# Six vector-engine exponentials per group, squared on GpSimd, in a one-core graph-attention kernel

## The chip, the cores and the metric

The kernel runs on one core of a Trainium2 chip. The core has TensorE (matmuls; the profile calls it PE, and its weight loads PEld), VectorE (DVE), ScalarE (ACT), GpSimd (POOL) and SyncE (SP, which here only issues DMAs). Each engine works through its own instruction list in order; semaphores order the engines among themselves. The metric is the device time of one execution in microseconds, and the median of several runs is quoted.

## The reference

Four layers work on a graph of 3,327 nodes with 128 features and a dense 3,327 x 3,327 matrix `adj`. Nearly all the time goes to the first layer, an attention with 128 heads of 8 elements each:

```python
q = (x @ Wq.T).reshape(d, n, h)          # d = 128 heads, n = 3327 nodes, h = 8
k = (x @ Wk.T).reshape(d, n, h)
v = (x @ Wv.T).reshape(d, n, h)
a = jnp.einsum('dnh,dmh->dnm', q, k) * d ** (-0.5)
a = a + adj + adj
a = softmax(a, axis=2)
out = einsum('dnm,dmh->dnh', a, v).reshape(n, h * d) @ Wo.T
```

So for every head and every pair of nodes there is one exponential: 128 x 3,327 x 3,327, some 1.4 billion. The other three layers multiply with `adj` a few times and take the last 800 us of the span.

## The kernel before

**Work and order.** The attention stage handles the nodes n in 7 chunks of up to 476 columns (`CW`), the heads in 32 groups of four (`NG`), and the nodes m in 26 tiles of 128, taken two at a time as 13 *pairs* per group (`q` = 0..12; rows `r` = 0 and 1 of a pair). That makes 7 x 32 = 224 groups and 2,912 pairs. The order of the instructions on every engine is written out by hand (`manual_schedule`): the loop over `i` at the end of the stage runs through *slots*, four to a pair, one for each head j. The index u counts pairs.

**Scores in place.** A pair owns two of seven PSUM banks of `S`. VectorE *seeds* a bank with adj minus a shift (`seed`, L645). TensorE adds the scores of head 0 (`scores`, L654), ScalarE takes exp(2x) of both rows in one instruction 952 columns wide (`exps`, L666), and then TensorE turns the bank from head j-1 to head j by adding q_j k_j - q_(j-1) k_(j-1), so that one seed serves four heads. For this `QS` holds q of head j beside the negated q of the head before. Every seventh pair has its banks at the two ends of the ring, and there ScalarE needs two instructions of 476 columns (L669) for each head. `values` (L713) multiplies the four heads' exponentials by V into bank `po`, two slots of matmuls after the last head.

**By hand.** In the pairs with q in `BY_HAND` = (0, 2, 5, 7, 10), *hand pairs* below, VectorE computes the exponential of row 1, head 0, by a polynomial, and ScalarE only does row 0 (476 columns) in that slot. `hand_exp` reads the raw score out of PSUM (L691, tile `h`), seeds the bank for the later heads (`seed(u, 1)`), and then runs four more instructions (L695 three times, L697), the last of which multiplies by `EA`, the exponential of adj minus shift. The loop spreads these: one in slot 3 of the hand pair, two in slot 0 of the next pair and one in its slot 3. A generator in `by_vector` holds the state. `heads_of` lets `values` use a hand-made exponential one pair later than the others.

**Other VectorE work.** In slot 1 the loop seeds row 1 of the *next* pair (`seed(u+1, 1)`), unless that is a hand pair, and in slot 2 row 0 of the pair after that. Both seeds of one bank wait until ScalarE has read the bank's former content. In slot 2 of the pair q = 2 the sums of the group before are copied out of `po` (`store`, L721). While the chunks run, 22 of the 26 squares of `adj` are also transposed piece by piece for later use (`Square`, `plan_squares`: L288, L292), three or four per chunk.

**Loads for the next group** (`loads`, on SP's queue): at q = 1 all keys (`load_k`, 16 DMAs into `KT`), q of head 0 (`load_q`) and V (`load_v`). At q = 3, 5 and 7 GpSimd negates q of head 0, 1 and 2 (`negate_q`, L570), and the next head's q is loaded over part of it. At q = 8 GpSimd spreads V (`spread_v`, L580) and reads one column of `KT` (`all_here`, L584), which the first scores of the next group wait for. In the last group of a chunk the next chunk's 26 tiles of `adj` are loaded too. GpSimd also issues the stores of the sums (L725).

## Time and profile before

| what | value |
|---|---|
| median of 3 runs | 10,983.07 us (10,979.53 to 10,989.63) |
| the profiled execution | 10,981.96 us, of which its span is 10,980.2 us |
| attention loop, first to last exponential | 462.5 to 10,168.1 us of the span |
| busy in that stretch: ACT, PE, DVE, POOL | 9,667.7, 9,609.5, 7,786.3, 1,290.0 us |
| granted TensorE clock in that stretch | 1.00 |
| DMA share in that stretch | 0.58, 96 GB/s |

A line of the page's costliest groups reads: source line, engine, operation, output tile <- input tiles, shapes, count | busy us, mean ns of one | idle time of that engine just before these instructions, and who ended it. The mean of one instruction contains its start and end, which overlap with the neighbours on ScalarE; what counts for the loop is the distance from start to start. A line of the timeline reads: start, length, engine, source line, operation, tiles, count, and in square brackets the idle time before it with who ended it; neighbouring instructions of one group are merged.

### The profile page before, as it was taken

The page shows a single profiled execution, that of the slowest core. Times are in us where ns is not written, and L with a number is a line of the kernel's source. Part 1 is how long each engine was busy: PE and PEld are TensorE (multiplying, and loading weights), DVE is VectorE, ACT ScalarE, POOL GpSimd, SP SyncE. Part 2 cuts the span into 40 slices and gives each one's busy share as a digit, 9 for nine tenths or more (in the row PEclk, how much of TensorE's full clock was granted, in tenths as well). Part 3 has the DMA queues.
Part 4 walks back from the last instruction along what each step waited for, and adds up shares of the span by engine and source line. Part 5 has one row for each costly group of instructions (what it writes and reads, how often), then busy time and mean ns, then how long its engine had stood idle before and what let it go on. Part 6 is the DMA issues. An engine that isn't in the chain of part 4 may idle for free. (4 is left out here: it accounts for less than half of the span.)

```text
span 10980.2 us, 204474 instructions
## 1 busy us (share of the span) xinstructions
PE 10533.5 (96%) x72876; PEld 3435.7 (31%) x72876; DVE 8487.1 (77%) x13503; ACT 10033.1 (91%) x13789; POOL 1529.1 (14%) x2477
## 2 busy tenths in 40 slices
PE   4599999999999999999999999999999999999889
PEld 2133333333333333333333333333323333333544
DVE  5588887888878887788887888878877777777655
ACT  3599999999999999999999999999999999999330
POOL 5011111111111111111111111111111111111101
PEclk7799999999999999999999999999999999999999
DMA  8766566565566565565556565565556555554668
GB/s 250 250 99 97 94 96 113 93 98 96 89 118 97 93 97 88 106 98 97 90 95 119 94 96 93 95 119 95 87 93 98 96 95 86 82 88 71 206 233 281
DMA packets 695339, 1256.98 MB, mean 114 GB/s; under 512 B 195218, under 2 KB 555049, under 8 KB 691244
## 3 DMA queue, kind: packets, MB, share of 16 engines
q1 hardware_dynamic: 644044, 1114.42, 55.7%
q0 software_dynamic: 50272, 129.37, 4.3%
q8 instruction: 587, 9.62, 0.4%
q14 instruction: 436, 3.57, 0.2%
HBM read 1096.53 MB, written 146.60 MB: 113 GB/s over the span
## 5 line engine op out<-in xcount | busy, mean ns | idle before, releaser
L666 ACT ACTIVATE e<-S 128x952 f32<-128x952 f32 (+1 forms) x9024 | 8357.9, 1099 | 36.7 <-PE S L654 29.4
L713 PE MATMUL po<-e,VA 128*9 128x476 f32 (+1 forms) x46592 | 5737.5, 564 | 33.0 <-DVE OS L721 12.3
L645 DVE TENSOR_TENSOR S<-a,shb 128x476 f32<-128x476 f32 (+1 forms) x5824 | 3937.9, 676 | 1447.6 <-ACT e L666 1059.4
L654 PE MATMUL S<-QS,KT 64*128 64x476 f32 (+1 forms) x22176 | 4528.6, 445 | 79.7 <-DMA a<-adjT 28.4
L654 PEld LDWEIGHTS S<-QS,KT 64*128 64x128 f32 x22176 | 2073.7, 184 | 5100.5 <-issue 1301.3
L669 ACT ACTIVATE e<-S 128x476 f32<-128x476 f32 (+1 forms) x4128 | 2467.5, 711 | 1.1 <-PE S L654 0.6
L695 DVE SCALAR_TENSOR_TENSOR e<-e,h 128x476 f32<-128x476 f32 (+1 forms) x2240 | 1497.8, 669 | 77.0
L713 PEld LDWEIGHTS po<-e,VA 128*9 128x9 f32 x46592 | 691.0, 88 | 1606.6 <-issue 1488.1
L570 POOL TENSOR_SCALAR QS<-QS 128x476 fp32r<-128x476 f32 (+1 forms) x672 | 485.6, 723 | 4312.1 <-DMA QS<-qS_d 2612.2
L725 POOL DMA_DIRECT2D oT_d<-OS x896 | 470.5, 530 | 3668.8 <-DVE OS L721 3625.5
L691 DVE TENSOR_SCALAR h<-S 128x476 f32<-128x476 f32 (+1 forms) x1120 | 728.0, 650 | 300.9 <-PE S L654 296.5
L697 DVE SCALAR_TENSOR_TENSOR e<-e,EA 128x476 f32<-128x476 f32 (+1 forms) x1120 | 759.6, 678 | 0.0
L695 DVE SCALAR_TENSOR_TENSOR e<-h 128x476 f32<-128x476 f32 (+1 forms) x1120 | 743.1, 663 | 0.0
L1107 PE MATMUL pu<-strip,y 128*128 128x512 f32 (+2 forms) x1456 | 600.5, 566 | 31.7 <-DVE y L968 14.8
L654 PE MATMUL S<-QZ,KT 64*128 64x476 f32 (+1 forms) x1120 | 493.4, 441 | 11.9 <-DVE S L645 10.5
L1107 PEld LDWEIGHTS pu<-strip,y 128*128 128x128 f32 (+1 forms) x1456 | 271.9, 191 | 305.8 <-issue 272.1
L1111 DVE TENSOR_REDUCE deg<-strip 128x1 f32<-128x1536 f32 (+1 forms) x104 | 193.8, 1881 | 63.7 <-DMA strip<-adjT 44.1
L580 POOL COPY VA<-VR 128x832 f32<-128x832 f32 x224 | 242.3, 1082 | 0.0
L654 PEld LDWEIGHTS S<-QZ,KT 64*128 64x128 f32 x1120 | 205.1, 183 | 92.2 <-DVE S L645 52.4
L288 DVE STREAM_TRANSPOSE cols<-rows 128x416 f32<-128x416 f32 x208 | 204.5, 988 | 30.3 <-DMA rows<-in_adj_dram 22.6
L1060 ACT COPY uT<-pu 128x512 f32<-128x512 f32 (+1 forms) x21 | 11.1, 555 | 222.6 <-PE pu L1107 222.6
L721 DVE COPY OS<-po 128x476 f32<-128x476 f32 (+1 forms) x224 | 146.3, 653 | 87.3 <-PE po L713 87.3
(255 smaller groups left out, 1958.6 us busy)
## 6 DMA issues: line engine op xcount, KB each, us to landing
KT<-kS_d SPq DMA_DIRECT2D x1792, 208.0 KB
KT<-kS_d SPq DMA_DIRECT2D x1792, 104.0 KB
VR<-v_d SPq DMA_DIRECT2D x224, 416.0 KB
QS<-qS_d SPq DMA_DIRECT2D x3072, 14.9 KB
QS<-qS_d SPq DMA_DIRECT2D x1536, 29.8 KB
adjT<-cols SPq DMA_DIRECT2D x26, 1664.0 KB
a<-adjT SPq DMA_DIRECT2D x156, 238.0 KB
strip<-adjT POOLq DMA_DIRECT2D x39, 895.5 KB, 5.1
```

The lines of the kernel that those rows point to most:

```text
L570: nc.gpsimd.tensor_scalar(QS[b][:, j + 1, :w], QS[b][:, j, :w].bitcast(F32), -1.0, 0.0, op0=ALU.mult, op1=ALU.add)
L580: nc.gpsimd.tensor_copy(VA[(c * NG + g) % 2][:, :, :, 0:H], v.rearrange("p j (t e) -> p t j e", e=H))
L645: touch(u, [r], nc.vector.tensor_tensor(bank(u, r), adj_of[c][2 * q + r][:, :w], shift_of[c][:, :w], op=ALU.subtract))
L654: x = nc.tensor.matmul(bank(u, r), KT[b][64 * r:64 * r + 64, max(0, j - 1), q * P:(q + 1) * P], q_s[64 * r:64 * r + 64, :w], start=hand an ...
L666: touch(u, (0, 1), nc.scalar.activation(e[:, :, :w], S[:, odd:even + 1, :w], AF.Exp, scale=2.0))
L669: touch(u, [r], nc.scalar.activation(e[:, 1 - r, :w], bank(u, r), AF.Exp, scale=2.0))
L691: touch(u, [1], nc.vector.tensor_scalar(s, bank(u, 1), EXP_ARG, None, op0=ALU.mult))
L695: nc.vector.scalar_tensor_tensor(e, s if k == 3 else e, EXP_C[k], s, op0=ALU.add, op1=ALU.mult)
L697: nc.vector.scalar_tensor_tensor(e, e, EXP_C[0], EA[pairs[u][2]][:, :w], op0=ALU.add, op1=ALU.mult)
L713: nc.tensor.matmul(po[32 * j:32 * j + H + 1, :w], VA[k % 2][:, 2 * pairs[v][2] + of, j, :], e_of[v, j][:, 1 - of, :w], start=(q == 0 and r ...
L725: nc.gpsimd.dma_start(oT_d[:, d * N + c * CW:d * N + c * CW + w], o[32 * j:32 * j + H + 1, :w])
L1107: nc.tensor.matmul(ps[:, :k], y[:m, t, :], s[:m, c * 4 * P - c0:c * 4 * P - c0 + k], start=(t == 0), stop=(t == NT - 1))
```

## The change

The hand pairs become q = 0, 2, 4, 6, 8 and 10, every second one. The polynomial has one VectorE instruction less: VectorE adds a constant while it reads the score (L691), GpSimd squares the result, and three VectorE instructions follow, of which the first waits for the square. None of them stands in the hand pair itself any more: two stand in slot 0 and one in slot 3 of the pair behind it. `heads_of` goes, and with it the later use of the hand-made exponential; the head-0 tile has 4 buffers in place of 5, and there are six `EA` tiles in place of five.

VectorE negates q, at q = 4, 6 and 8, at the end of slot 0, which is behind `seed(u, 1)` and ahead of `seed(u+1, 1)`. Keys and q are loaded head by head at q = 1, 4, 6 and 8, q first. V is loaded at q = 9, and `spread_v` and `all_here` stand at q = 12. The load of an `adj` square stands three pairs later, its two transposes at q = 10 and 12 in place of 4 and 9.

```diff
-BY_HAND = (0, 2, 5, 7, 10)
+QK_AT = (1, 4, 6, 8)
+BY_HAND = (0, 2, 4, 6, 8, 10)
...
-            nc.gpsimd.tensor_scalar(QS[b][:, j + 1, :w], QS[b][:, j, :w].bitcast(F32),
-                                    -1.0, 0.0, op0=ALU.mult, op1=ALU.add)
+            nc.vector.tensor_scalar(QS[b][:, j + 1, :w], QS[b][:, j, :w].bitcast(F32), -1.0, None, op0=ALU.mult)
...
-                e = e_of[u, j] = e_e.tile([P, 2, CW], F32, name=f"e{j}", bufs=(5, 4, 3, 2)[j])
+                e = e_of[u, j] = e_e.tile([P, 2, CW], F32, name=f"e{j}", bufs=(4, 4, 3, 2)[j])
...
-                touch(u, [1], nc.vector.tensor_scalar(s, bank(u, 1), EXP_ARG, None, op0=ALU.mult))
+                touch(u, [1], nc.vector.tensor_scalar(z, bank(u, 1), EXP_C[0], None, op0=add))
+                nc.gpsimd.tensor_tensor(e, z, z, op=mult)
                 seed(u, 1)
                 yield
-                for k in (3, 2, 1):
-                    nc.vector.scalar_tensor_tensor(e, s if k == 3 else e, EXP_C[k], s, op0=ALU.add, op1=ALU.mult)
-                    yield
-                nc.vector.scalar_tensor_tensor(e, e, EXP_C[0], EA[pairs[u][2]][:, :w], op0=ALU.add, op1=ALU.mult)
+                v(z, e, EXP_C[1], z, op0=add, op1=add)
+                yield
+                v(e, e, EXP_C[2], z, op0=add, op1=mult)
+                yield
+                v(e, e, EXP_C[3], EA[pairs[u][2]][:, :w], op0=add, op1=mult)
...
-                    if q == 1:
-                        load_k(*nxt)
-                        load_q(*nxt, 0)
+                    if q in QK_AT:
+                        j = QK_AT.index(q)
+                        if j:
+                            negate_q(*nxt, j - 1)
+                        load_q(*nxt, j)
+                        load_k(*nxt, j)
+                    if q == 9:
                         v_of[k + 1] = load_v(*nxt)
-                    if q in (3, 5, 7):
-                        negate_q(*nxt, q // 2 - 1)
-                        load_q(*nxt, q // 2)
-                    if q == 8:
+                    if q == 12:
                         spread_v(*nxt, v_of.pop(k + 1))
                         here[k + 1] = all_here(*nxt)
...
-                        plan(u, sq.load, j)
-                        plan(u + 4, sq.turn, j, 0)
-                        plan(u + 9, sq.turn, j, 1)
+                        plan(u + 3, sq.load, j)
+                        plan(u + 10, sq.turn, j, 0)
+                        plan(u + 12, sq.turn, j, 1)
...
-                for k in range(0 if at % 3 else 1 if at else 0 if by_hand(i // 4) else 2):
+                for k in range(0 if at % 3 or by_hand(i // 4) else 1 if at else 2):
```

More of the change, by code (lines that the diff above doesn't have):

```diff
@@ L46 @@
 NOTHING = -1.0e30
-EXP_C = (0.9999990463256836, 2.2162604331970215, 2.4563632011413574, 1.8291265964508057)
-EXP_ARG = 0.9023826718330383
-BY_HAND = (0, 2, 5, 7, 10)
+EXP_C = (0.25674915313720703, 0.05050157010555267, 1.8002841472625732, 0.8117094039916992)
+EXP_LEAD = -0.2054332047700882
+QK_AT = (1, 4, 6, 8)
+BY_HAND = (0, 2, 4, 6, 8, 10)
 LN_EPS = 1e-5
@@ L539, in gnn_kernel, with load_k @@
         po = e_ps.tile([P, 512], F32, name="po")
-        def load_k(c, g):
+        def load_k(c, g, j):
             b = (c * NG + g) % 2
-            for j in range(4):
-                d = 4 * g + j
-                k0, nk = max(0, j - 1), 1 if j in (0, 3) else 2
-                for r in range(2):
-                    r0 = 64 * r + 32 * (1 - j % 2)
-                    k_d = kS_d[:, :, d, r * NQ * P:(r + 1) * NQ * P].rearrange("i e n -> (i e) n")
-                    for i in range(2):
-                        nc.sync.dma_start(KT[b][r0 + 16 * i:r0 + 16 * i + 16, k0:k0 + nk, :].bitcast(F32),
-                                          k_d.unsqueeze(1).to_broadcast([16, nk, NQ * P]))
+            d = 4 * g + j
+            k0, nk = max(0, j - 1), 1 if j in (0, 3) else 2
+            for r in range(2):
+                r0 = 64 * r + 32 * (1 - j % 2)
+                k_d = kS_d[:, :, d, r * NQ * P:(r + 1) * NQ * P].rearrange("i e n -> (i e) n")
+                for i in range(2):
+                    nc.sync.dma_start(KT[b][r0 + 16 * i:r0 + 16 * i + 16, k0:k0 + nk, :].bitcast(F32),
+                                      k_d.unsqueeze(1).to_broadcast([16, nk, NQ * P]))
         def load_q(c, g, j):
@@ L677, in shifted @@
                 w = width_of(c)
-                nc.vector.tensor_tensor(EA[q][:, :w], adj_of[c][2 * q + 1][:, :w], shift_of[c][:, :w], op=ALU.subtract)
+                nc.vector.scalar_tensor_tensor(EA[q][:, :w], adj_of[c][2 * q + 1][:, :w], EXP_LEAD, shift_of[c][:, :w],
+                                               op0=ALU.add, op1=ALU.subtract)
             def bare(c, q):
@@ L688, in hand_exp @@
                 w = width_of(pairs[u][0])
-                s = e_h.tile([P, CW], F32, name="h")[:, :w]
+                v, add, mult = nc.vector.scalar_tensor_tensor, ALU.add, ALU.mult
+                z = e_h.tile([P, CW], F32, name="h")[:, :w]
                 e = e_of[u, 0][:, 0, :w]
-                touch(u, [1], nc.vector.tensor_scalar(s, bank(u, 1), EXP_ARG, None, op0=ALU.mult))
+                touch(u, [1], nc.vector.tensor_scalar(z, bank(u, 1), EXP_C[0], None, op0=add))
+                nc.gpsimd.tensor_tensor(e, z, z, op=mult)
                 seed(u, 1)
                 yield
-                for k in (3, 2, 1):
-                    nc.vector.scalar_tensor_tensor(e, s if k == 3 else e, EXP_C[k], s, op0=ALU.add, op1=ALU.mult)
-                    yield
-                nc.vector.scalar_tensor_tensor(e, e, EXP_C[0], EA[pairs[u][2]][:, :w], op0=ALU.add, op1=ALU.mult)
-            def heads_of(u, r):
-                first = (u, r)
-                if by_hand(u) and r == 1:
-                    first = (u + 1, 0)
-                elif by_hand(u - 1):
-                    first = (u, 1) if r == 0 else (u - 1, 1)
-                return [first] + [(u, r)] * 3
+                v(z, e, EXP_C[1], z, op0=add, op1=add)
[3 more added lines that the diff above has]
+                v(e, e, EXP_C[3], EA[pairs[u][2]][:, :w], op0=add, op1=mult)
             def values(u, r):
@@ L711, in values @@
                 w, k = width_of(c), c * NG + g
-                for j, (v, of) in enumerate(heads_of(u, r)):
-                    nc.tensor.matmul(po[32 * j:32 * j + H + 1, :w], VA[k % 2][:, 2 * pairs[v][2] + of, j, :],
-                                     e_of[v, j][:, 1 - of, :w], start=(q == 0 and r == 0),
+                for j in range(4):
+                    nc.tensor.matmul(po[32 * j:32 * j + H + 1, :w], VA[k % 2][:, 2 * q + r, j, :],
+                                     e_of[u, j][:, 1 - r, :w], start=(q == 0 and r == 0),
                                      stop=(q == NQ - 1 and r == 1))
@@ L770, in gnn_kernel @@
             v0 = load_v(0, 0)
-            load_k(0, 0)
             load_q(0, 0, 0)
+            for j in range(4):
+                load_k(0, 0, j)
             shift_of[0] = load_shift(0)
```

## The prediction

> **What bounds the kernel now.** I read the page's busy shares and costliest groups first, then the busy times of the attention loop alone, then the timeline of single pairs.

> ```profile
> PE 10533.5 (96%) x72876; PEld 3435.7 (31%) x72876; DVE 8487.1 (77%) x13503; ACT 10033.1 (91%) x13789; POOL 1529.1 (14%) x2477
> ...
> L666 ACT ACTIVATE e<-S 128x952 f32<-128x952 f32 (+1 forms) x9024 | 8357.9, 1099 | 36.7 <-PE S L654 29.4
> ...
> L645 DVE TENSOR_TENSOR S<-a,shb 128x476 f32<-128x476 f32 (+1 forms) x5824 | 3937.9, 676 | 1447.6 <-ACT e L666 1059.4
> ...
> L570 POOL TENSOR_SCALAR QS<-QS 128x476 fp32r<-128x476 f32 (+1 forms) x672 | 485.6, 723 | 4312.1 <-DMA QS<-qS_d 2612.2
> ...
> L691 DVE TENSOR_SCALAR h<-S 128x476 f32<-128x476 f32 (+1 forms) x1120 | 728.0, 650 | 300.9 <-PE S L654 296.5
> ```

> ScalarE is idle for 36.7 us ahead of its main line in the whole span, and in the loop it is busy 9,667.7 of 9,705.5 us. VectorE's seeds wait over 1,000 us for ScalarE, so VectorE is not the bound on average. From start to start a 952-column activation takes 845 ns (median in the trace) and a 476-column one 447. A pair without hand work therefore costs ScalarE at least 4 x 845 = 3,380 ns, or 8 x 447 = 3,576 in the one pair of seven whose banks lie apart: mean 3,408. A hand pair costs 447 + 3 x 845 = 2,982 or 7 x 447 = 3,129: mean 3,003. A group's floor is 8 x 3,408 + 5 x 3,003 = 42.28 us. The trace has 9,705.6 / 224 = 43.33. The missing 1.05 us lie in few places: by position the mean pair takes 3.14, 3.40, 3.14, 3.73, 3.45, 3.06, 3.43, 3.11, 3.44, 3.41, 3.13, 3.46, 3.41 us (q = 0 to 12, 43.31 in all). Hand pairs lose about 0.1 each, since TensorE needs 1.54 us for the matmuls of two slots and a hand pair gives it 3.0 for four. The pair q = 3 loses 0.32: the copy of `po` at q = 2 makes the seeds late.

> **What is saved.** One more pair of 3,408 becomes one of 3,003: 0.405 us a group, 91 us over 224 groups, if all else stands.

> **The polynomial.** VectorE's share falls from 650 + 4 x 650 to 650 + 3 x 650 ns for each exponential (L691 and L695 when undisturbed), so six cost 15.6 us a group where five cost 16.3. Spread over two pairs it gives VectorE 2.7 us in every pair; before, a hand pair had 3.3 with its seeds, more than it lasted. That is a gain, and it alone would end the stall at q = 3, for pair 4 no longer needs its row-1 seed early.

> **The square.** The trace has no GpSimd square of this size, but sums of squares in the first stage:

> ```profile
> L369 POOL TENSOR_TENSOR sq<-sq 128x512 f32<-128x512 f32 x52 | 65.9, 1268 | 28.5 <-ACT sq L367 27.4
> L369 POOL TENSOR_TENSOR sq<-sq 128x256 f32<-128x256 f32 x52 | 37.6, 722 | 4.2
> ```

> That is 2.13 ns a column, so 1,191 ns for 476 columns (an estimate from these rows). Its length is not the trouble, since its result is needed two microseconds later; what it does to VectorE is. Of the timeline at a hand pair q = 10 into which GpSimd's work falls by chance:

> ```profile
> 6822.28 0.65 DVE L691 TENSOR_SCALAR h<-S 128x476 f32<-128x476 f32 x1 [0.37 <-PE S L654]
> ...
> 6822.97 0.66 DVE L645 TENSOR_TENSOR S<-a,shb 128x476 f32<-128x476 f32 x1
> ...
> 6824.02 0.88 POOL L580 COPY VA<-VR 128x832 f32<-128x832 f32 x1
> ...
> 6824.28 1.90 DVE L645 TENSOR_TENSOR S<-a,shb 128x476 f32<-128x476 f32 x2 [0.65 <-ACT e L666]
> ...
> 6825.02 1.17 PE L654 MATMUL S<-QS,KT 64*128 64x476 f32 x4
> ```

> Two seeds take 1.90 us where they take 1.43 elsewhere, and the four score matmuls behind them 1.17 where an undisturbed pair shows 0.70. Counted over the trace, a seed or polynomial step (two operands in SBUF) that begins beside a GpSimd instruction on SBUF does not run until that one ends, and then ends 502 ns later (380 cases beside L570). The other way round, L570, 586 ns long alone, ends 441 ns after the VectorE instruction that it met (298 cases). So they exclude each other, and only GpSimd's first 145 ns are free.

> Now the hand pair's own clock, from q = 5 (medians, from ScalarE's first start in that pair): L691 from -0.28 to 0.38, `seed(u, 1)` to 1.07, then VectorE waits for ScalarE until 1.46, `seed(u+1, 1)` ends at 2.15, the next pair's scores start at 2.46, and the next pair at 3.01. The square starts about 0.12 behind L691 (so long after VectorE's L292 does GpSimd's L284 start); the seed, 0.03 behind, goes first. The square thus runs from 1.07 to 1.07 + 1.19 - 0.145 = 2.12, and `seed(u+1, 1)` ends at 2.12 + 0.50 = 2.62. Scores start 0.05 later, take 0.48, and ScalarE starts 0.04 behind: 3.20. The trace confirms it: hand pairs in which that seed ended at 2.5 to 2.7 took 3.18 us at q = 7 (5 pairs) and 3.31 at q = 10 (12 pairs), against 3.03 with the seed at 2.2 to 2.35 (65 pairs at q = 10). I take 3.22 for q = 0 and 2, and 3.25 for q = 10, where half the groups now have a transpose (988 ns, L288) between the seeds.

> **The negation on VectorE** stands just ahead of `seed(u+1, 1)` at q = 4, 6 and 8. GpSimd's L570 goes, and with it collisions at q = 7 to 11. Two bounds: L288, one operand in SBUF, takes 995 ns beside L570 and 993 alone, so such an instruction need not wait for the square, and the negation (0.65 like L691) would lie beside it for nothing. But L226, one operand and 3,328 columns, takes 1,850 ns where two-operand L222 takes 3,609: it moves two columns at a time, as if on both operands' paths, and what uses both waits. Then it runs behind the square, some 0.41 us long (L167 takes 180 ns for 14 columns, L226 1,850 for 3,328: 0.504 a column), and the seed ends up to 0.45 later. I take the waiting, by the kinship with L226. The five hand pairs at q = 10 whose seed ended beyond 2.7 took 3.47 on average: 3.47 for q = 6 and 8. At q = 4 the copy of `po` comes on top: L691 is reached about 0.5 late (copy 0.65, seed 0.66, three steps 2.0, seed 0.66 behind q = 2's late seed), so 3.47 + 0.25 = 3.72, between no loss and q = 3's 0.32 of today.

> [...]

> **Loads and arrival check.** Today GpSimd negates head 0 some 20 us after pair 1 began, as 16 key DMAs (12.8 us from first to last issue) stand ahead of it; nobody waits for it. On VectorE such a wait would hold the seeds. With q first: 6 issues take 2.1 us (9 take 3.1) and land 0.8 to 1.9 behind the last, so 4 to 5 us after the negation before, where two pairs give 6.6: hidden, by about 1.5 us. In a chunk's last group the `adj` tiles share the queue, and negations come 6 to 7 us apart already; a few us in each of 6 groups. `all_here` ends 31 us after pair 1 began, 8 us early (median); now V is issued at q = 9 and the check stands at q = 12. V lands some 4 us after its issue and both copies take 1.5, so normally some 3 us stay. In the 22 groups with a square's store (1,664 KB, 8 us) at q = 8, ahead of the last keys and V, nothing to 4 us are lost. Together 0 to 100 us; I take 30. `heads_of` and the tile counts cost nothing: the last step ends 6 slots ahead of its matmul. The sixth `EA` costs ScalarE 7 x 0.49 = 3 us.

> **Sum.** A group: 7 pairs of 3.41 (as q = 1, 9 and 12 today) = 23.87, hand pairs 3.22 + 3.22 + 3.72 + 3.47 + 3.47 + 3.25 = 20.35, in all 44.22, or 0.91 above 43.31. 224 x 0.91 = 204; with 3 and 30, 237 us on the profiled 10,982, which lies 1 us below the median of the runs: **11,220 us**.

> **Rivals.**
> - *The square costs nothing* (ends faster). It decides if the square leaves VectorE's path before `seed(u+1, 1)` is due, at 1.46 to 1.7 us, that is if it holds VectorE 0.4 us shorter than L369's rows say or TensorE runs 0.3 us further ahead. Then hand pairs take 3.08 to 3.10, q = 4 3.30, and a group 42.7: 224 x -0.61 + 33 = -104: 10,880; with no stall by loads 10,850. For it: VectorE idles 0.4 us there today. Against it: the collisions above.
> - *The square costs, the negation doesn't*: q = 6 and 8 at 3.22, q = 4 at 3.47, 0.75 a group less than the sum: 11,052, and 10,980 to 11,130 with the loads' bounds.
> - *VectorE waits for DMAs*: a landing 3 us later than worked out in every group at one negation: more than 600 us on top, over 11,800. Against it: the 1.5 us of room, and a slower loop gives more.

> **Chances.** Forecast 0.43 (11,130 to 11,360, its own range), square free 0.28, negation free 0.24 (a quarter of it within 0.2% of now), DMA waits 0.05. The range leaves out the DMA case and the best end: 10,840 to 11,360. Measurements tell 0.2% (22 us) from no change: faster 0.28, same 0.06, slower 0.66.

> **What would show it.** In the new profile: L645 at `seed(u+1, 1)` some 0.3 us longer than 0.66 in hand pairs, with idle TensorE or ScalarE released by VectorE; mean of the GpSimd square well over 1.19 us (it waits for a seed first); the negation's mean at 0.41 or 0.65, longer if it waits; DVE waits on DMA QS; TensorE waits on GpSimd's `seen` in 22 groups. Hand pairs at 3.1 us would refute the sum.

## The result, and the profile after

The changed kernel takes **11,669.51 us** (median of 4 runs, 11,652.62 to 11,672.93) where the kernel before takes 10,985.74 (4 runs beside them): 1.062 times as long, 95% interval 1.0602 to 1.0638. The forecast said slower, but 11,220 us and no more than 11,360. The profiled run took 11,671.56 us; its attention loop lasts 10,400 us, and the one before 9,706, so the loop has the whole difference.

The busy shares and the costliest groups of the kernel after:

```profile
PE 10771.8 (92%) x72876; PEld 3498.9 (30%) x72876; DVE 8914.0 (76%) x13958; ACT 10026.2 (86%) x13764; POOL 2894.3 (25%) x3149
...
PE 54%; DMA 20%; DVE 8%; ACT 5%; SPq 4%; issue 4%; DVEq 0%; POOL 0%; POOLq 0%; ACTq 0%
PE po L706 28%; PE S L653 21%; DMA QS<-qS_d 9%; DMA KT<-kS_d 7%; PE pu L1102 4%; ACT e L665 4%; DMA adjT<-cols 3%; DVE S L644 2%; SPq L564 2%; DVE QS L570 2%; DVE OS L714 1%; SPq L562 1%; DVE h L692 1%; ACT e L668 1%; SPq L551 1%
...
L665 ACT ACTIVATE e<-S 128x952 f32<-128x952 f32 (+1 forms) x8832 | 8106.1, 1028 | 464.1 <-PE S L653 434.0
...
L644 DVE TENSOR_TENSOR S<-a,shb 128x476 f32<-128x476 f32 (+1 forms) x5824 | 4034.7, 693 | 1135.8 <-ACT e L665 807.8
...
L693 POOL TENSOR_TENSOR e<-h 128x476 f32<-128x476 f32 (+1 forms) x1344 | 1846.9, 1374 | 6334.9 <-DVE h L692 5535.6
...
L692 DVE TENSOR_SCALAR h<-S 128x476 f32<-128x476 f32 (+1 forms) x1344 | 875.7, 652 | 455.2 <-PE S L653 414.1
...
L570 DVE TENSOR_SCALAR QS<-QS 128x476 fp32r<-128x476 f32 (+1 forms) x672 | 613.2, 912 | 524.8 <-DMA QS<-qS_d 524.8
```

(Some lines moved up by one: the seed is now L644, the scores L653, ScalarE's exponentials L665 and L668, the values L706, spreading V L579, the check L583.) ScalarE is as busy as before (10,026 us against 10,033) but idle for 464 us ahead of its main line, where it was idle for 37. A fifth of the chain that ended last is DMA: q of the next group, its keys, and the stores of `adj` squares. The negation L570 waits 524.8 us for q, and VectorE's first step of the polynomial (L692) 414 us for TensorE, 296 before. Counted pair by pair over the trace, from start to start of a pair's first exponential, means over 222 groups (the forecast's column is the one of its sum; pairs it did not name singly are its 3.41):

| q | 0 | 1 | 2 | 3 | 4 | 5 | 6 | 7 | 8 | 9 | 10 | 11 | 12 | group |
|---|---|---|---|---|---|---|---|---|---|---|---|---|---|---|
| before | 3.14 | 3.40 | 3.14 | 3.72 | 3.45 | 3.06 | 3.42 | 3.11 | 3.44 | 3.41 | 3.13 | 3.46 | 3.41 | 43.30 |
| forecast | 3.22 | 3.41 | 3.22 | 3.41 | 3.72 | 3.41 | 3.47 | 3.41 | 3.47 | 3.41 | 3.25 | 3.41 | 3.41 | 44.22 |
| after | 3.39 | 3.42 | 3.19 | 3.41 | 3.31 | 3.44 | 3.32 | 3.44 | **4.56** | **4.14** | 3.16 | 3.42 | **4.21** | 46.42 |

Of the 3.12 us a group, q = 8, 9 and 12 hold 2.65, and q = 0 another 0.25. This is how q = 8 comes about in group 100, from the timeline of the kernel after (start, length, engine, line; in brackets the idle time before and who ended it):

```profile
5143.32 1.72 SPq L551 DMA_DIRECT2D KT<-kS_d  x4
...
5144.92 1.18 DVE L570 TENSOR_SCALAR QS<-QS 128x476 fp32r<-128x476 f32 x1
...
5146.13 0.32 SPq L562 DMA_DIRECT2D QS<-qS_d  x1
...
5147.56 1.69 SPq L564 DMA_DIRECT2D QS<-qS_d  x2
...
5154.76 0.41 DVE L570 TENSOR_SCALAR QS<-QS 128x476 fp32r<-128x476 f32 x1 [3.04 <-DMA QS<-qS_d]
...
5155.80 1.04 PE L653 MATMUL S<-QS,KT 64*128 64x476 f32 x3 [2.22 <-DVE S L644]
...
5156.48 1.82 ACT L665 ACTIVATE e<-S 128x952 f32<-128x952 f32 x2 [2.60 <-PE S L653]
```

Head 1's keys, which stand at q = 4 in SP's list, are issued from 5143.32 (first line, four DMAs of 208 KB). The negation of head 1 ends at 5146.10, six issues for q of head 2 follow until 5149.25, and the last of these lands at 5154.54 (the semaphore update that the negation waits for): 8.4 us after the negation, not the 4 to 5 of the forecast. The median over 220 groups is 7.3 us from the first of these issues to the last landing, where the kernel before has 3.3. VectorE stands still for 3.04 us; behind its negation stand the seeds, behind them TensorE (2.22) and ScalarE (2.60). And it does not end there. Windows of the same stretch (length, then busy us and instructions of PE, PEld, DVE, ACT and POOL, then the granted TensorE clock, the DMA share and GB/s):

```profile
5154.00:5155.80 1.80, 0.00 (x2) 0.01 (x2) 0.98 (x2) 0.00 (x0) 0.00 (x0) 1.00 1.06 126
5155.80:5157.00 1.20, 1.20 (x7) 0.51 (x11) 1.16 (x2) 0.52 (x1) 0.00 (x0) 0.56 0.90 105
...
5158.00:5159.00 1.00, 1.00 (x6) 0.50 (x4) 0.67 (x2) 0.30 (x1) 0.00 (x0) 0.50 0.77 78
...
5160.00:5161.00 1.00, 1.00 (x12) 0.30 (x4) 0.04 (x1) 1.00 (x2) 0.00 (x0) 1.00 0.63 180
```

TensorE is idle from 5153.58 to 5155.80, and then its clock is granted at one half for some 3.4 us: it is "busy" throughout, but from one set of four matmuls of L706 to the next 0.76 us pass (median of 136 in this loop at half clock) where 0.40 pass at full clock (5,652). So the pair behind this stall, q = 9, is slow too (4.55 us). Before, the loop ran at 1.00 but for one stretch of 6.8 us.

Not every stall has this behind it. Of the 96 groups in which the negation at q = 8 waited 2.0 to 3.2 us, 47 had half clock in q = 8 or 9, and q = 9 took 4.77 us on average there; in the other 49 it took 3.41. It goes with where the stall lies: in this loop the granted clock changed 207 times, only on a grid of 3.413 us (within 0.01), and of the 84 grid periods at full clock in which TensorE was idle for 1.5 us or more (gaps over 0.3 us added up), 83 were followed by one at half; of the 40 with 1.2 to 1.5 us, 19; of the 2,753 with less, one. In all, 64 groups have the negation at q = 8 and half clock there or in q = 9; they hold 86 of the 161 us by which the q = 9 of all groups exceed 3.42. Another 68 lie in the 24 groups in which the negation came only during q = 9.

The waits of the kernel after (engine, tile and line; what it waited for; us in all, times, longest):

```profile
POOL VA L579 <- DMA VR<-v_d: 910.1, 212, 17.2
...
DVE QS L570 <- DMA QS<-qS_d: 524.8, 225, 21.2
...
ACT e L665 <- PE S L653: 434.0, 413, 11.6
...
PE S L653 <- POOL seen L583: 160.9, 28, 11.2
```

The last line is q = 12: in the 22 groups with a square's store at q = 8 (1,664 KB ahead of the last keys and V), that pair takes 11.09 us on average, and 3.41 in the others, the six last of a chunk aside (3.9 to 5.7).

### The profile page after: what moved, and what is told of

The parts are those of the page before. It is cut to its first block, busy times and chain, and to the rows that moved or that the text cites. A ratio compares the mean times of both kernels' runs of the same rounds, so it can differ in the third digit from the quotient of the medians.

```text
span 11669.8 us, 207519 instructions
## 1 busy us (share of the span) xinstructions
PE 10771.8 (92%) x72876; PEld 3498.9 (30%) x72876; DVE 8914.0 (76%) x13958; ACT 10026.2 (86%) x13764; POOL 2894.3 (25%) x3149
## 3 DMA queue, kind: packets, MB, share of 16 engines
q14 instruction: 454, 3.72, 0.1%
## 4 chain that ended last, share of the span: by engine, by line
PE 54%; DMA 20%; DVE 8%; ACT 5%; SPq 4%; issue 4%; DVEq 0%; POOL 0%; POOLq 0%; ACTq 0%
PE po L706 28%; PE S L653 21%; DMA QS<-qS_d 9%; DMA KT<-kS_d 7%; PE pu L1102 4%; ACT e L665 4%; DMA adjT<-cols 3%; DVE S L644 2%; SPq L564 2%; DVE QS L570 2%; DVE OS L714 1%; SPq L562 1%; DVE h L692 1%; ACT e L668 1%; SPq L551 1%
## 5 line engine op out<-in xcount | busy, mean ns | idle before, releaser
L665 ACT ACTIVATE e<-S 128x952 f32<-128x952 f32 (+1 forms) x8832 | 8106.1, 1028 | 464.1 <-PE S L653 434.0
L706 PE MATMUL po<-e,VA 128*9 128x476 f32 (+1 forms) x46592 | 5848.8, 574 | 30.7 <-DVE OS L714 8.0
L653 PE MATMUL S<-QS,KT 64*128 64x476 f32 (+1 forms) x21952 | 4600.6, 447 | 538.0 <-DVE S L644 322.5
L644 DVE TENSOR_TENSOR S<-a,shb 128x476 f32<-128x476 f32 (+1 forms) x5824 | 4034.7, 693 | 1135.8 <-ACT e L665 807.8
L653 PEld LDWEIGHTS S<-QS,KT 64*128 64x128 f32 x21952 | 2102.1, 188 | 5568.1 <-issue 1566.3
L693 POOL TENSOR_TENSOR e<-h 128x476 f32<-128x476 f32 (+1 forms) x1344 | 1846.9, 1374 | 6334.9 <-DVE h L692 5535.6
L668 ACT ACTIVATE e<-S 128x476 f32<-128x476 f32 (+1 forms) x4288 | 2405.5, 639 | 274.6 <-PE S L653 273.0
L692 DVE TENSOR_SCALAR h<-S 128x476 f32<-128x476 f32 (+1 forms) x1344 | 875.7, 652 | 455.2 <-PE S L653 414.1
L706 PEld LDWEIGHTS po<-e,VA 128*9 128x9 f32 x46592 | 691.9, 88 | 1736.3 <-issue 1617.9
L570 DVE TENSOR_SCALAR QS<-QS 128x476 fp32r<-128x476 f32 (+1 forms) x672 | 613.2, 912 | 524.8 <-DMA QS<-qS_d 524.8
L698 DVE SCALAR_TENSOR_TENSOR e<-e,h 128x476 f32<-128x476 f32 (+1 forms) x1344 | 888.1, 661 | 46.0
L700 DVE SCALAR_TENSOR_TENSOR e<-e,EA 128x476 f32<-128x476 f32 (+1 forms) x1344 | 900.7, 670 | 0.0
L696 DVE SCALAR_TENSOR_TENSOR h<-e,h 128x476 f32<-128x476 f32 (+1 forms) x1344 | 876.5, 652 | 0.0
L653 PE MATMUL S<-QZ,KT 64*128 64x476 f32 (+1 forms) x1344 | 615.4, 458 | 5.4 <-DVE S L644 4.0
L579 POOL COPY VA<-VR 128x832 f32<-128x832 f32 x224 | 239.1, 1068 | 1014.2 <-DMA VR<-v_d 910.1
L653 PEld LDWEIGHTS S<-QZ,KT 64*128 64x128 f32 x1344 | 249.6, 186 | 120.2 <-DVE S L644 20.4
```

What stands on the lines that cost most here:

```text
L570: nc.vector.tensor_scalar(QS[b][:, j + 1, :w], QS[b][:, j, :w].bitcast(F32), -1.0, None, op0=ALU.mult)
L644: touch(u, [r], nc.vector.tensor_tensor(bank(u, r), adj_of[c][2 * q + r][:, :w], shift_of[c][:, :w], op=ALU.subtract))
L653: x = nc.tensor.matmul(bank(u, r), KT[b][64 * r:64 * r + 64, max(0, j - 1), q * P:(q + 1) * P], q_s[64 * r:64 * r + 64, :w], start=hand an ...
L665: touch(u, (0, 1), nc.scalar.activation(e[:, :, :w], S[:, odd:even + 1, :w], AF.Exp, scale=2.0))
L668: touch(u, [r], nc.scalar.activation(e[:, 1 - r, :w], bank(u, r), AF.Exp, scale=2.0))
L692: touch(u, [1], nc.vector.tensor_scalar(z, bank(u, 1), EXP_C[0], None, op0=add))
```

## The experiments

Theory **L**, later called **Q**: the loss is waits for the next group's loads, and what counts is what is queued ahead of q and which engine does the waiting. Rival **S**: my forecast's terms, the square and the negations as such. Positions are means over 222 groups, counted as above.

### Keys in one go again

```diff
                         load_q(*nxt, j)
-                        load_k(*nxt, j)
-                    if q == 9:
+                    if q == 1:
+                        for j in range(4):
+                            load_k(*nxt, j)
                         v_of[k + 1] = load_v(*nxt)
```

> The kernel after, with all keys of the next group and its V issued at q=1 again, behind q of head 0; negations stay on VectorE at q=4, 6, 8, the arrival check at q=12. Theory L (the loss is load waits: q of head 2 lands late because it queues behind 832 KB of head 1's keys): the wait of the negation at q=8 goes, q=8, 9 and 0 fall from 4.56, 4.14 and 3.39 us to about 3.3, 3.4 and 3.1; only the groups with a square's store may still wait at q=12; 11,000 to 11,200 us against 11,670. Theory S (my forecast: the square and the negations themselves cost some 200 us, the loads 30): 11,600 to 11,670, no change beyond 70 us.

Measured: **11,989.03 us**, 1.092 of before. Both missed. The pair q = 8 fell to 3.44 as theory L had it, but q = 6 rose to 6.41 and q = 7 to 4.76. The waits of this kernel:

```profile
DVE QS L570 <- DMA QS<-qS_d: 825.1, 186, 20.3
```

All keys and V now stand ahead of q of *head 1*, so its negation at q = 6 waits. The mechanism holds; I had counted only what is ahead of head 2. To put much in the queue early helped only an engine that could afford to wait (GpSimd, 2,612 us before).

### Negation by GpSimd again, nothing else

```diff
-            nc.vector.tensor_scalar(QS[b][:, j + 1, :w], QS[b][:, j, :w].bitcast(F32), -1.0, None, op0=ALU.mult)
+            nc.gpsimd.tensor_scalar(QS[b][:, j + 1, :w], QS[b][:, j, :w].bitcast(F32),
+                                    -1.0, 0.0, op0=ALU.mult, op1=ALU.add)
```

> The kernel after, with the three negations of q on GpSimd again, at the same pairs q=4, 6, 8; all loads as in after. Theory L, that it matters who waits: GpSimd, not VectorE, waits for q of head 2, its next square is 6.6 us away, so q=8 and q=9 fall by about 2 us together, while the check at q=12 still waits in groups with a store: 11,150 to 11,300 us. Theory S: the negations' own cost goes (about 0.5 us a group, 110 us), and GpSimd's negation of 1 us holds VectorE up instead: 11,550 to 11,670.

Measured: **11,392.06 us**, 1.038 of before. q = 8 and 9 fall to 3.08 and 3.40, but q = 12 rises from 4.21 to 5.34 and q = 0 from 3.39 to 3.83. The waits:

```profile
POOL VA L580 <- DMA VR<-v_d: 1447.2, 188, 18.3
...
PEld S L654 <- POOL seen L584: 671.8, 222, 14.0
...
POOL QS L570 <- DMA QS<-qS_d: 612.8, 225, 20.8
```

GpSimd waits longer for q than VectorE did (613 us against 525), and nobody minds, since the next square is 6.6 us away. But V and the last keys do not come sooner, and a group that is not held at q = 8 reaches the check at q = 12 sooner: half of what is saved at q = 8 and 9 turns into that wait, which comes in nearly every group now. That is why theory L expected too much. The hand pairs q = 2, 4, 6 and 8 take 3.05 to 3.09 here, with the square in them.

### The square's store later

```diff
-                    for k, f in ((0, sq.gather), (1, sq.back), (7, sq.finish), (8, sq.store)):
+                    for k, f in ((0, sq.gather), (1, sq.back), (7, sq.finish), (11, sq.store)):
```

> The kernel after, with the store of a finished square of adj (1,664 KB) issued at q=11 in place of q=8, nothing else. Theory L (the check at q=12 waits for the last keys and V, which queue behind that store in 24 groups, 7 us each, and the next group starts with a clock of one half): 11,450 to 11,520 us. Theory S (loads cost 30 us in all): 11,640 to 11,670.

Measured: **11,520.54 us**, 149 less than after; in the 22 store groups (L's 24 counts two that have no square) q = 12 falls from 11.09 to 6.34. That is half a microsecond above theory L's range: some 2.9 us of the 7.7 stay in each store group. For S it is out of reach.

### Only the loads, in the kernel before

The kernel before, with `load_k`, `negate_q`, `loads` and the plan of the squares as in after; five exponentials and the old polynomial stay.

> The kernel before (five exps by VectorE, the old polynomial, the order of values as it was) with only the loads of after: q and keys head by head at q=1, 4, 6, 8, V at 9, spreading and arrival check at 12, negation by VectorE, the later loads and turns of adj. Theory L: the waits come with the loads whatever computes: 11,550 to 11,750 us against 10,986 before. Theory S: 11,000 to 11,100.

Measured: **11,424.15 us**, 1.040 of before. The waits come without the square (q = 8 at 4.15, q = 12 at 4.27), but the time is 126 us below L's lowest. The line of the negation in this kernel:

```profile
L570 DVE TENSOR_SCALAR QS<-QS 128x476 fp32r<-128x476 f32 (+1 forms) x672 | 270.5, 403 | 238.1 <-DMA QS<-qS_d 237.6
```

Here it takes 403 ns, beside no GpSimd square, against 912 on average in after, and its wait for q is 238 us in place of 525. The two fit together, since the next head's q can only be issued when the negation is done: what holds a negation also delays the next load. That this is all of the missing 126 us is not shown.

### Only the computation, with the loads of before

The kernel after, with `load_k`, `loads`, the GpSimd negation (q = 3, 5, 7) and the check (q = 8) of before.

> The kernel after with the loads, the negations by GpSimd (q=3, 5, 7) and the check (q=8) of before: the six exps with GpSimd's squares alone. Theory Q (a wait for q of the next group costs what is queued behind it): before, GpSimd waited 2,612 us in all for q and nobody minded; now the squares of q=4, 6, 8 stand behind those waits, and VectorE's chain behind the squares, so the groups grow by 3 to 9 us at q=4 to 8: 11,600 to 13,000 us. Theory S (my forecast's terms for the square alone, without loads): 11,100 to 11,250.

Measured: **13,015.82 us**, 1.186 of before and 16 us above theory Q's range: q = 6 takes 11.84. The waits:

```profile
POOL QS L571 <- DMA QS<-qS_d: 3504.8, 662, 27.9
...
DVE h L698 <- POOL e L695: 1825.0, 225, 16.3
```

GpSimd waited 2,612 us for q in the kernel before too, at no cost. Now the squares stand behind those waits in its order, and VectorE's polynomial behind the squares. So the new computation can't do with the old loads: with squares on GpSimd the negations, or the loads that they wait for, have to move, which my prediction did not see.

### Loads spaced out, on GpSimd and on VectorE

```diff
-QK_AT = (1, 4, 6, 8)
+QK_AT = (1, 4, 7, 10)
...
-                        load_k(*nxt, j)
-                    if q == 9:
+                        for j in {1: (0, 1), 7: (2, 3)}.get(q, ()):
+                            load_k(*nxt, j)
+                    if q == 4:
                         v_of[k + 1] = load_v(*nxt)
...
-                    for k, f in ((0, sq.gather), (1, sq.back), (7, sq.finish), (8, sq.store)):
+                    for k, f in ((0, sq.gather), (1, sq.back), (7, sq.finish), (12, sq.store)):
```

The first of the two also has the GpSimd negation shown above; the second leaves it on VectorE.

> The kernel after with three pairs between the links of the q chain (q=1, 4, 7, 10), each q ahead of the large transfers of its pair (keys of heads 0 and 1 at q=1, V at 4, keys of heads 2 and 3 at 7), the square's store at q=12, negations by GpSimd. Theory Q: no wait is left on the path, and the group falls to the 42.4 us that the undisturbed pairs of the second experiment add up to: 10,760 to 10,900 us, faster than before. Theory S: 11,000 to 11,200, since the squares remain.

> The same loads as spaced_gpsimd, with the negations on VectorE as in after: the difference of the two is the price of negating on VectorE beside a square, without a wait for q. Theory Q: 0.2 to 0.8 us a group, 50 to 180 us more than spaced_gpsimd, 10,850 to 11,050 us; 600 us of the loss are gone. Theory S: 11,150 to 11,350.

Measured: **10,880.14 us** on GpSimd, 0.991 of before (0.9892 to 0.9925): faster than both kernels. On VectorE **11,061.91 us**, 1.007 of before. In the first, ScalarE's idle time is gone:

```profile
L666 ACT ACTIVATE e<-S 128x952 f32<-128x952 f32 (+1 forms) x8832 | 8279.6, 1123 | 27.0 <-PE S L654 25.9
```

The same exponentials with the same squares, only with other loads: 789 us less than after. The second lies 12 us above theory Q's range. It has the negations on VectorE as after has, at q = 4, 7 and 10 in place of 4, 6 and 8, and still wins back 608 us of the 684; VectorE's wait for q is down to 49.6 us:

```profile
L570 DVE TENSOR_SCALAR QS<-QS 128x476 fp32r<-128x476 f32 (+1 forms) x672 | 552.3, 822 | 52.0 <-DMA QS<-qS_d 49.6
```

So that much of the loss is load waits. The other 182 us between the two kernels stand at q = 4 (3.30 against 3.07) and q = 10 and 11 (7.46 against 6.61), less 0.25 at q = 0 and 12. The timeline of spaced_vector at q = 10:

```profile
4870.25 1.38 POOL L693 TENSOR_TENSOR e<-h 128x476 f32<-128x476 f32 x1 [5.07 <-DVE h L692]
...
4870.71 1.00 DVE L289 STREAM_TRANSPOSE cols<-rows 128x416 f32<-128x416 f32 x1
...
4871.58 0.88 POOL L579 COPY VA<-VR 128x832 f32<-128x832 f32 x1
4871.63 1.08 DVE L570 TENSOR_SCALAR QS<-QS 128x476 fp32r<-128x476 f32 x1
4872.64 1.41 DVE L644 TENSOR_TENSOR S<-a,shb 128x476 f32<-128x476 f32 x2
```

With V landed early, GpSimd spreads it straight behind the square, and the negation beside it takes 1.08 us; the first seed behind it ends 3.5 us after ScalarE's first start in the pair (4869.74), where it ends at 2.5 at q = 10 of after (median). At q = 7, without a square, the negations take 401 ns (median).

### The square left out

spaced_gpsimd with this edit:

```diff
-                nc.gpsimd.tensor_tensor(e, z, z, op=mult)
...
-                v(z, e, EXP_C[1], z, op0=add, op1=add)
+                v(e, z, EXP_C[1], z, op0=add, op1=add)
```

> spaced_gpsimd with GpSimd's square left out: the first step of the polynomial reads z in its place, so the value of these exps is another. The difference from spaced_gpsimd is the whole price of the square. Theory Q: 0 to 40 us less, since the undisturbed hand pairs took 3.05 to 3.09 us with it. Theory S: my forecast had 0.1 us in each of six pairs and more where a negation stood, so 130 to 200 us less.

Measured: **10,920.56 us**, 40 *more* than with the square. So both theories missed: taking out the square, with what moves when it goes, gains nothing, and S's 130 to 200 us are refuted. Where the 40 come from is not settled. They stand at q = 4 (3.29 against 3.07), and GpSimd's negations, no longer held behind a square, start anywhere from q = 3 to 11 and not at q = 4, 6 and 10; that they meet worse instructions there is only argued.

### Half the keys

```diff
+                    x = NQ * P if c == 0 and g < 2 else 6 * P
-                    nc.sync.dma_start(KT[b][r0 + 16 * i:r0 + 16 * i + 16, k0:k0 + nk, :].bitcast(F32),
-                                      k_d.unsqueeze(1).to_broadcast([16, nk, NQ * P]))
+                    nc.sync.dma_start(KT[b][r0 + 16 * i:r0 + 16 * i + 16, k0:k0 + nk, :x].bitcast(F32),
+                                      k_d[:, :x].unsqueeze(1).to_broadcast([16, nk, x]))
```

> The kernel after with 6 of 13 tiles of every key row loaded from the third group on, by as many DMAs issued at the same places; the other tiles keep older keys, so it leaves out part of the loads and its scores are others. Theory Q (the q of head 2 lands late because the keys' bytes move ahead of it on the same queue): the waits at q=8 and 9 go, and those of the check shrink: 11,050 to 11,250 us. Rival D (it lands late by the number of issues and their fixed latency, not by bytes): 11,550 to 11,650.

Measured: **11,096.19 us**, 573 less than after with the same instructions in the same places. q = 8 and 9 fall to 3.27 and 3.44. The negation's line:

```profile
L571 DVE TENSOR_SCALAR QS<-QS 128x476 fp32r<-128x476 f32 (+1 forms) x672 | 782.5, 1165 | 41.2 <-DMA QS<-qS_d 40.6
```

Its wait for q falls from 524.8 to 40.6 us, so it is the keys' bytes that q waits behind, not the number of issues. From its first issue q of head 2 lands in 3.4 us here (median), in 7.3 in after. That it is the keys ahead of q and not those behind it, spaced_vector shows: there 1,248 KB of keys follow right behind q of head 2, and it lands in 3.3 us. With fewer bytes ahead of q on SP's queue, 484 us of waiting are gone.

### Negations in the pairs between, and the square on VectorE

```diff
-QK_AT = (1, 4, 6, 8)
+QK_AT = (1, 3, 7, 9)
```

with V at q = 3, and keys and store as in the spaced kernels; negations on VectorE. The second kernel also has

```diff
-                nc.gpsimd.tensor_tensor(e, z, z, op=mult)
                 seed(u, 1)
+                nc.vector.tensor_tensor(e, z, z, op=mult)
```

> As spaced_vector, but with the links of the q chain at q=1, 3, 7, 9, so that every negation by VectorE stands in a pair without a hand exp, 400 ns as at q=7 of spaced_vector, and V at q=3. Theory Q: the price of negating on VectorE (182 us between spaced_vector and spaced_gpsimd) is GpSimd's square or copy beside it, so it goes whole: 10,800 to 10,900 us. Rival V (VectorE has no room for them anywhere): 11,000 to 11,080.

> odd_vector with the six squares by VectorE, behind the seed, in place of GpSimd. Theory Q (hand pairs of 3.05 us are set by ScalarE's exps, VectorE has room): within 60 us of odd_vector, either way. Rival V (VectorE is the bound in the hand pairs): 6 times 0.65 us a group, up to 870 us more, 11,200 to 11,700.

Measured: **10,981.30 us** (0.9997 of before, 0.9988 to 1.0006) and **11,021.36 us**. Of the first theory Q is right on the negation's length and 81 us off in the time. Its negation:

```profile
L570 DVE TENSOR_SCALAR QS<-QS 128x476 fp32r<-128x476 f32 (+1 forms) x672 | 271.6, 404 | 136.6 <-DMA QS<-qS_d 133.7
```

404 ns on average, and in the groups with no piece of an `adj` square, the last of each chunk aside, a group takes 42.55 us (spaced_gpsimd 42.71). But the 22 store groups take 47.97, with q = 10 at 7.13: the negation at q = 9 waits again for q of head 2, two pairs behind its issue at q = 7, and V and a small store with its own wait stand ahead of it. Against the 42.78 of all other groups that is 22 x 5.2 = 114 us. The second kernel prices GpSimd's help: 3.9 us more of VectorE's time in each group end as 40 us in all, so VectorE has room, as Q said.

### Five exponentials in place of six

spaced_gpsimd with `BY_HAND = (0, 2, 4, 6, 8)`.

> spaced_gpsimd with five exps per group by VectorE (q=0, 2, 4, 6, 8), the one at q=10 back on ScalarE. Theory Q (a hand pair takes 3.05 to 3.2 us, another 3.41): 0.2 to 0.35 us a group more, 10,920 to 10,970 us. Rival V (the sixth is held up by VectorE and GpSimd as much as it saves): within 30 us of spaced_gpsimd, 10,850 to 10,910.

Measured: **10,969.17 us**, 89 more than spaced_gpsimd; q = 10 takes 3.44 in place of 3.17, q = 0 takes 3.34 in place of 3.23. The sixth exponential is worth what it should be.

## Why the prediction was wrong

**What was right.** The direction. The saving's ceiling (91 us for the sixth exponential; five_hands gives 89). The stall at q = 3 ends (3.72 to 3.41). The negation waits for the square, by L226's kinship and not by L288's row: it takes 1,184 ns (median) at q = 4 and 6, against 408 alone (q = 8). A seed that meets GpSimd ends 0.52 us after it (worked out: 0.50).

**The failed step** is in "Loads and arrival check": q lands "0.8 to 1.9 behind the last" issue, "so 4 to 5 us after the negation before, where two pairs give 6.6: hidden, by about 1.5 us". The landing times were read from the kernel before, where q of head 1 and later had nothing new ahead of them. The change puts 832 KB of head 1's keys between q of head 1 and q of head 2. In group 100 q landed 5.3 us behind its last issue, 8.4 behind the negation. The issues themselves were held too: the last two took 1.69 us where two take 0.65. I had it that the order "q first" settles this; it does so within one stage, but q of head 2 stands behind the keys of the stage before. What I took as 30 us is 608 by spaced_vector, and halving the keys alone gives back 573.

**The check** was to lose "nothing to 4 us" in 22 groups; it lost 7.7 us in each of them at q = 12, and the pair behind it, the first of the next group, is slow too (5.35 us on average, 3.14 behind the others). Moving the store alone gave back 149.

**The rival that came true** is the third, VectorE waiting for DMAs, 3 us at one negation of every group, more than 600 us. The mechanism was the right one and so was its price: 225 waits of 2.3 us on average, and some 600 us with what they bring. I gave it 0.05. Against it I had set "the 1.5 us of room", which is the failed step itself. It ended at 11,670 and not "over 11,800" because the rest of the sum, on top of which I put it, did not come.

**The square** was priced too high, and that hid part of the miss: without load waits the group is not 44.22 us but, by an estimate, about 43.2. q = 1 to 11 take 36.73 us in half_keys; with 3.06 for q = 0 (spaced_vector) and 3.41 for q = 12 (as before) that is 43.20, no loss against 43.30. The term that was mis-sized is the square's length, "1,191 ns for 476 columns", taken from L369's rows; the order, "the seed, 0.03 behind, goes first", held. Counted over the trace of after at q = 6 (medians, from ScalarE's first start) and shown by group 100:

```profile
5143.66 0.65 DVE L692 TENSOR_SCALAR h<-S 128x476 f32<-128x476 f32 x1
5143.94 0.60 ACT L668 ACTIVATE e<-S 128x476 f32<-128x476 f32 x1
5144.35 0.66 DVE L644 TENSOR_TENSOR S<-a,shb 128x476 f32<-128x476 f32 x1
...
5144.46 1.38 POOL L693 TENSOR_TENSOR e<-h 128x476 f32<-128x476 f32 x1 [5.32 <-DVE h L692]
...
5144.92 1.18 DVE L570 TENSOR_SCALAR QS<-QS 128x476 fp32r<-128x476 f32 x1
...
5146.02 1.42 DVE L644 TENSOR_TENSOR S<-a,shb 128x476 f32<-128x476 f32 x2
```

the square's row starts at 0.52, while the seed runs, and ends at 1.90 (5144.46 + 1.38, less 5143.94), 0.22 earlier than worked out. Over all 1,344 squares it ends 0.83 us behind that seed (median); with the 0.145 that may lie beside it, the square is 0.98 us long and not 1.19. The three squares of the spaced kernels that start beside no VectorE instruction take 976 to 982 ns. `seed(u+1, 1)` ends at 2.42 without a negation and 2.74 with one, and the pairs take 3.02 to 3.10 (3.22 at q = 2, as forecast) and 3.31, where I had 3.22 to 3.25 and 3.47. At q = 4 the additional 0.25 for the copy of `po` did not come at all (3.31 against 3.72). Together this is 1.02 us a group, 228 us too much. The profiled run took 690 us more than the one before, where the sum had 237, so the loads and what they bring were some 680 too little.

**Not seen at all:** the half clock behind many of the stalls, which holds over half of what q = 9 lost, and that the old loads and the new computation exclude each other (13,016 us).

## What to carry to other kernels

When an instruction that waits for a DMA moves from an idle engine to a busy one, list what is queued ahead of that DMA *in the new order*, in bytes, and give the landing time those bytes (q of head 2 landed 7.3 us after its first issue behind 832 KB of keys, 3.4 behind 384); landing times of the old order are no evidence. An idle engine that waits thousands of microseconds for loads (GpSimd, 2,612 before) does useful work by waiting, and giving it a second job takes that away (13,016 us in compute_only). A wait of two or three microseconds on TensorE's path can cost more than its length: behind about half of such waits here (47 of 96) the clock fell, and the next pair took 1.4 us longer (4.77 against 3.41). Spacing the loads (here three pairs between the links of the chain, large transfers behind small ones, the store behind the check) brought a kernel that was 6.2% slower to 0.7% slower, and with the negations back on GpSimd to 0.9% faster, with the same computation.
